# Attention 2 of a two-layer graph kernel: four destination blocks a turn in place of two, and another use of PSUM

## Chip, core and metric

The kernel runs on one core of a Trainium2 chip. The metric is the device time of one execution in microseconds (us). A core has a matrix engine (TensorE, PE in the profile, with its weight loads as PEld), VectorE (DVE), ScalarE (ACT), GpSimd (POOL) and SyncE (SP, which here only issues transfers). Each works through its own list of instructions in a fixed order, and waits at an instruction until what it needs is there.

## What is computed

Two pre-norm residual layers over a graph of 6250 nodes with 128 features and 200000 edges sorted by destination. The first layer is a two-stage graph attention network; the second a convolution over edges. The part that matters here is the second attention stage, with one head (feat has 64 columns before W2):

```python
feat = (x @ W).reshape(num_nodes, H, D)
el = jnp.sum(feat * attn_l[None], axis=-1)
er = jnp.sum(feat * attn_r[None], axis=-1)
e = jax.nn.leaky_relu(el[src] + er[dst], NEG_SLOPE)
ee = jnp.exp(e - m[dst])
s = jax.ops.segment_sum(ee, dst, num_segments=num_nodes)
msg = feat[src] * (ee / s[dst])[:, :, None]
rst = jax.ops.segment_sum(msg, dst, num_segments=num_nodes)
```

then `x = x + rst`, a layer norm, a ReLU, and two linear maps of the result for the convolution.

## The kernel before

Nodes are cut into 49 blocks of 128 (NB). The program has three stages one after the other: tables, edge counts and attention 1 (0 to 2430 us of the profiled execution), attention 2 (2430 to 3014 us), and the convolution (from 3014 us to the end).

Attention 2 is dense. Attention 1 has left in DRAM, for each destination block, a matrix of edge counts: how many edges run from each of the 6272 sources to each of its 128 destinations. The leaky ReLU has two branches, so each count is split in two: `up` where el + er is positive, `down` where it isn't. Then `up` and `down`, as weights, are multiplied with two prepared tables (`rhs2`, 196 columns each: three bf16 pieces of 65 values, and a column of ones that counts edges).

The loop before (from line 1156) takes two destination blocks a group, 25 groups (24 of two blocks, one of one). A group does this:

- SP loads the counts `ct` of both blocks for all 49 source blocks, 8 transfers of 392 KB (line 1162).
- PE spreads er over the partitions (`pe`, line 1164, one small PSUM bank of two in `ps_sm`), and ACT copies it to `erb` (line 1167, two buffers).
- Seven steps, each over 7 source blocks (HS). In a step ACT makes 7 `ramp` rows of 256 columns (line 1181: Relu of erb times 2^60 plus a bias, so 0 or huge), DVE makes `up` as the smaller of ramp and count (1185) and `down` as count minus up (1186), and PE multiplies 28 weights of 128x128 with 196 columns (1190), `up` first for both blocks, then `down`. `ramp`, `up` and `down` have two buffers each.
- The sums stand in a tile `big` of two banks (two buffers, so four banks), and DVE takes them out with four instructions a block (1198 to 1202).

After every second group `finish2` (lines 1105 to 1151) is made for the four blocks just done. It is a generator of nine pieces, of which one is taken after each step of the groups that follow, so that its work is spread between theirs: shares on DVE (512 to 515), transposes of g on PE (312) with a copy on ACT (314), a product with W2 (1115), the sum into `xt` on DVE (1116), norm statistics (291, 292), a root on ACT (301), eight `h` on ACT (1127, 1128), and, twice for two blocks each, transposes (312), a copy on DVE (314), a product with `lin` (1136), a copy to `t3` on ACT (1139) and two updates of `xt` a block on DVE (1144, 1146). Its end is two writes by SP (table3 at 1150, xtd at 1151). Its PSUM comes from the one bank of `ps_bank`.

PSUM has eight banks: four for `big`, two for `ps_sm`, one for `ps_bank`, one kept for sums elsewhere. In the second group `load_inputs` (1092 to 1094) loads x into `xt` and lets POOL add a bias to all of it; in the fifth `load_tiles` brings two tables for the convolution. The convolution's first gather from table3 can start once the last `finish2` has been written.

The order of instructions on each engine is not that of the source: a scheduler of the framework sorts them when the program is built, by its own estimate of when each can start. Buffers that are reused become waits. So where an instruction stands in its engine's list has to be read from the built program.

Of the kernel before, what the change touches and what calls it, by code (L numbers as in the profile page):

```python
# [30 lines left out]
F32 = mybir.dt.float32  # L31
# [11 lines left out]
P = 128  # L43
# [23 lines left out]
def gnn_kernel(ctx: ExitStack, tc: tile.TileContext, x, src, dst, attr4, attr8,  # L67
# [978 lines left out]
    ps_big = ps_two.enter_context(tc.tile_pool(name="ps_big", bufs=2, space=PSUM))  # L1046
    ps_sm = ps_two.enter_context(tc.tile_pool(name="ps_sm2", bufs=2, space=PSUM))
    ps_bank = ps_two.enter_context(tc.tile_pool(name="ps_bank2", bufs=1, space=PSUM))
# [50 lines left out]
    with tc.tile_pool(name="att2", bufs=1) as pool, tc.tile_pool(name="dense", bufs=2) as dense, \  # L1099
# [54 lines left out]

        behind = iter(())
        for b0 in range(0, NB, 2):
            n = min(2, NB - b0)
            ct = dense.tile([P, 2, NQ, NB, QN], BF16, name="ct")
            pe = small()
            for k in range(n):  # L1160
                for quarter in range(NQ):
                    (nc.sync if k == 0 or b0 else nc.scalar).dma_start(
                        ct[:, k, quarter].rearrange("p h d -> p (h d)"), counts[b0 + k][quarter])
                nc.tensor.matmul(pe[:, k * P:(k + 1) * P], er2[:, b0 + k, :].to_broadcast([P, P]), ident,
                                 start=True, stop=True)
            erb = dense.tile([P, 2 * P], F32, name="erb")
            nc.scalar.copy(erb[:, :n * P], pe[:, :n * P])
            if b0 == 0:
                for h0 in range(0, NB, HS):
                    nc.sync.dma_start(rhs2[:, h0:h0 + HS], rhs2d[:, h0:h0 + HS])  # L1170
            if b0 == 2:
                load_inputs()
            acc = big().rearrange("p (k a) c -> p k (a c)", k=2)
            if b0 == 8:
                load_tiles(pool)
            for h0 in range(0, NB, HS):
                ramp = dense.tile([P, HS, 2 * P], BF16, name="ramp")
                up = dense.tile([P, HS, 2 * P], BF16, name="up")
                down = dense.tile([P, HS, 2 * P], BF16, name="down")
# [3 lines left out]
                c = ct[:, :n, :, h0:h0 + HS, :].rearrange("p k a h d -> p h (k a) d")  # L1183
# [3 lines left out]
                for j, m in ((0, up), (1, down)):  # L1187
                    for h in range(HS):
                        for k in range(n):
                            nc.tensor.matmul(acc[:, k, j * C2:(j + 1) * C2], m[:, h, k * P:(k + 1) * P],  # L1190
                                             rhs2[:, h0 + h, j, :],
                                             start=h0 + h + j == 0, stop=h0 + h + j == NB)
                next(behind, None)
            parts = dense.tile([P, 2, 2, R2], F32, name="parts")
            acc = acc[:, :n, :2 * C2].rearrange("p k (j c) -> p k j c", j=2)
            for k in range(n):
                b = b0 + k
                nc.vector.tensor_reduce(parts[:, k], acc[:, k, :, :3 * R2].rearrange("p j (s f) -> p j f s", s=3),
                                        axis=AX.X, op=OP.add)
                nc.vector.tensor_reduce(deg[:, b:b + 1], acc[:, k, :, C2 - 1], axis=AX.X, op=OP.add)  # L1200
                nc.vector.tensor_scalar(parts[:, k, 1, :], parts[:, k, 1, :], pq2[:, b, 1:2], None, op0=OP.mult)
                nc.vector.scalar_tensor_tensor(acc2[:, b, :], parts[:, k, 0, :], pq2[:, b, 0:1], parts[:, k, 1, :],
                                               op0=OP.mult, op1=OP.add)
            if b0 % 4 == 2 or b0 + n == NB:
                deque(behind, 0)
                behind = finish2(b0 // 4 * 4, b0 + n - b0 // 4 * 4)
# [6 lines left out]
        def all2():  # L1213
            load_inputs()
            for b0 in range(0, NB, 4):
# [274 lines left out]
```

## Time and profile before

| what | value |
|---|---|
| runs of the kernel | 5505.89, 5550.96, 5581.69 us; median 5550.96 |
| profiled execution, its own time | 5588.02 us |
| its span, first to last instruction | 5586.3 us, mean granted TensorE clock 0.72 |
| busy in attention 2, 2430 to 3014 us (584 us) | ACT 543.5, PE 502.6, PEld 451.5, DVE 481.0, POOL 14.0 us |
| granted TensorE clock in that stretch | 0.96 (0.68 before it, 0.70 after it) |
| transfers in that stretch | 164 GB/s, 48% of the 16 transfer engines |
| ramps (line 1181) | 1225, 491.8 us busy |
| pair products (line 1190) | 4802, 480.2 us busy |
| `up` and `down` (lines 1185, 1186) | 175 each, 386.4 us busy |

Busy times of PE overlap with themselves, since matmuls are pipelined and each is counted with its way through the array. In the views, "[idle before <-releaser]" is the time an engine stood still ahead of an instruction and what ended it; xN is a number of instructions merged into a row.

### The profile page before, as it was taken

Reading aid. Unit: us, or ns where it says so; the run is one execution under the profiler, and the core shown is the slowest. Engines: PE = TensorE matmul, PEld = TensorE weight load, DVE = VectorE, ACT = ScalarE, POOL = GpSimd, SP = SyncE. Lnnn points to the kernel's source line nnn. Section 1 sums busy time; section 2 is a strip of 40 time slices with the busy share of each in tenths; the row PEclk is TensorE's granted clock in tenths of the full one; section 3 lists DMA queues with packets and bytes.
Section 4 is the critical chain, followed back from the end, with each engine's and each line's share of the span. In section 5 each row is a group of like instructions: output and inputs, shape, how many; then the busy total and the mean of one; then the engine's idle time right before and its main releaser. Section 6 shows DMA issues by size and latency. Waiting matters only on the chain. (4 is left out here: it accounts for less than half of the span.)

```text
span 5586.3 us, 66809 instructions
## 1 busy us (share of the span) xinstructions
PE 3395.3 (61%) x22075; PEld 2519.0 (45%) x22076; DVE 3498.1 (63%) x5531; ACT 2900.8 (52%) x6921; POOL 2639.6 (47%) x2684
## 2 busy tenths in 40 slices
PE   3124554644555545569995566676667666677676
PEld 2124444544444445558884334344434344444444
DVE  4255555655656655668885566666666666666667
ACT  2024655754655656669995344444444444444444
POOL 2655545545345445310003555555556556555553
PEclk9998555655666556669997676767767666767667
DMA  4243433433334434454442111111111111111111
GB/s 105 60 125 98 120 109 110 137 104 108 110 113 118 118 101 118 115 188 151 163 165 70 45 48 47 46 49 48 48 47 49 46 48 49 48 47 49 47 48 30
DMA packets 348033, 480.97 MB, mean 86 GB/s; under 512 B 190602, under 2 KB 236208, under 8 KB 343695
## 3 DMA queue, kind: packets, MB, share of 16 engines
q1 hardware_dynamic: 199014, 238.86, 14.2%
q0 software_dynamic: 85776, 147.31, 11.2%
q10 hardware_dynamic: 62872, 90.28, 4.6%
q8 instruction: 181, 2.97, 0.2%
q14 instruction: 190, 1.55, 0.1%
HBM read 367.21 MB, written 108.97 MB: 85 GB/s over the span
## 5 line engine op out<-in xcount | busy, mean ns | idle before, releaser
L319 POOL DMA_INDIRECT G<-table,srcc x1563 | 1475.4, 944 | 1556.8 <-issue 676.6
L319 POOL DMA_INDIRECT G<-table,srcw x1054 | 1091.9, 1036 | 987.3 <-DVE w L362 384.4
L1300 PE MATMUL whole<-halves,ohr 128*128 128x512 f32 x1563 | 798.7, 647 | 24.3 <-issue 23.3
L885 ACT ACTIVATE ramp<-erb,sel 128x256 bf16<-128x256 f32 x1764 | 756.5, 499 | 1.9 <-DVE up L887 1.6
L1252 ACT ACTIVATE hid<-big 128x512 f32<-128x512 f32 x392 | 233.9, 597 | 951.5 <-PE big L1250 419.5
L780 ACT CAST ca<-small 128x392 bf16<-128x392 f32 x784 | 350.2, 482 | 644.3 <-remote 413.0
L778 PE MATMUL small<-key,lo 128*128 128x98 bf16 x3136 | 339.0, 260 | 484.3 <-ACT ca L780 213.3
L1300 PEld LDWEIGHTS whole<-halves,ohr 128*128 128x128 f32 x1563 | 418.1, 283 | 438.2 <-issue 373.7
L1250 PE MATMUL big<-a8t,wm_sb 16*128 16x512 f32 x392 | 294.5, 840 | 394.8 <-issue 346.6
L1274 ACT ACTIVATE g<-G,a 128x128 f32<-128x128 f32 x1563 | 506.9, 401 | 11.2 <-DMA G<-table,srcc 9.6
L1181 ACT ACTIVATE ramp<-erb,sel 128x256 bf16<-128x256 f32 (+1 forms) x1225 | 491.8, 499 | 23.5 <-DVE up L1185 16.8
L778 PEld LDWEIGHTS <-lo 128*128 128x128 bf16 x3136 | 262.4, 128 | 533.5 <-issue 523.0
L767 DVE TENSOR_TENSOR lo<-slots,turned 128x2048 bf16<-128x2048 bf16 x196 | 239.5, 1222 | 418.5 <-remote 206.0
L1293 DVE TENSOR_TENSOR halves<-mess,halves 128x1024 fp32r<-128x1024 f32 x196 | 239.1, 1220 | 350.6 <-ACT halves L1287 201.2
L1250 PE MATMUL big<-hid,wm_sb 128*128 128x512 f32 x392 | 356.7, 1011 | 112.4 <-ACT hid L1252 99.0
L905 PE MATMUL up<-rc,up 128*128 128x102 bf16 x3528 | 323.5, 268 | 144.8 <-DVE up L887 106.4
L1258 PE MATMUL big<-wtp_sb,hid 64*128 64x128 f32 x3126 | 289.4, 331 | 142.6 <-issue 79.0
L1258 PEld LDWEIGHTS big<-wtp_sb,hid 64*128 64x128 f32 x3126 | 244.2, 229 | 246.9 <-issue 140.0
L377 PE MATMUL whole<-halves,ohr 128*128 128x136 f32 x1054 | 248.1, 388 | 173.1 <-issue 80.0
L905 PEld LDWEIGHTS <-up 128*128 128x128 bf16 x3528 | 272.9, 131 | 176.5 <-DVE up L887 127.3
L887 DVE TENSOR_TENSOR up<-ramp,ctc 128x1792 bf16<-128x1792 bf16 x252 | 273.8, 1087 | 97.2 <-ACT ramp L885 64.2
L377 PEld LDWEIGHTS whole<-halves,ohr 128*128 128x128 f32 x1054 | 218.3, 294 | 185.2 <-issue 84.5
(294 smaller groups left out, 6252.9 us busy)
## 6 DMA issues: line engine op xcount, KB each, us to landing
counts<-ca ACTq DMA_DIRECT2D x196, 392.0 KB
ct<-counts SPq DMA_DIRECT2D x192, 392.0 KB
rc<-rhs SPq DMA_DIRECT2D x63, 717.5 KB
oht<-dlow SPq DMA_DIRECT2D x31, 1088.0 KB
ctc<-counts SPq DMA_DIRECT2D x504, 56.0 KB
G<-table,srcc POOLq DMA_INDIRECT x1563
G<-table,srcw POOLq DMA_INDIRECT x1054
a8t<-attr_rows SPq DMA_DIRECT2D x391, 16.0 KB
```

The source lines that it names most:

```text
L319: nc.gpsimd.indirect_dma_start(out=G[:, c, :], out_offset=None, in_=table, in_offset=bass.IndirectOffsetOnAxis(ap=idx[:, c:c + 1], axis=0))
L377: nc.tensor.matmul(acc, oh[:, c, :], ms[:, c].rearrange("e s f -> e (s f)"), start=start and c == 0, stop=stop and c == n - 1)
L778: nc.tensor.matmul(ps[:, k * NKEY:(k + 1) * NKEY], lo[:, a, :, r], ky[:, a, :, r], start=True, stop=True)
L780: nc.scalar.copy(ca[:, :, i * W:(i + WBANK) * W].rearrange("p h (k d) -> p h k d", d=W), ps[:, :WBANK * NKEY].rearrange("p (k h d) -> p h ...
L885: nc.scalar.activation(ramp[:, i, :n * P], erb[:, h, :n * P], AF.Relu, bias=sel1[:, h0 + i, h:h + 1], scale=STEEP)
L887: nc.vector.tensor_tensor(up[:, :, :n * P].rearrange("p h (a d) -> p h a d", d=QN), ramp[:, :, :n * P].rearrange("p h (a d) -> p h a d", d ...
L905: nc.tensor.matmul(ups[k][:, h], up[:, i, k * P:(k + 1) * P], by_head[:, i, :, h, :], start=h0 + i + h == 0, stop=h0 + i + h == NB + H1 - 2)
L1181: nc.scalar.activation(ramp[:, h, :n * P], erb[:, :n * P], AF.Relu, bias=sel2[:, h0 + h, :], scale=STEEP)
L1250: nc.tensor.matmul(ph, w, (hid[-1] if j else x)[:, :npr * P], start=True, stop=True)
L1258: nc.tensor.matmul(pw[:, c, :], hid[1][half, j * P:(j + 1) * P], wtp_sb[half].rearrange("x p u -> x (p u)"), start=True, stop=True)
L1274: nc.scalar.activation(g0[:, c], G[:, c, :], AF.Copy, scale=a0[:, c, :])
L1300: nc.tensor.matmul(acc, oh[:, c, :], ms[:, c].rearrange("e s h i u -> e (s h i u)"), start=start, stop=stop)
```

## The change

Attention 2 is cut otherwise. All edits are between the pools of the stage and its end.

- Groups, called turns, have four blocks; block 0 alone goes first (49 = 1 + 12 x 4), where the odd block was last before. `ramp`, `up`, `down` and `erb` have 512 columns; `erb` has one buffer.
- The counts come in three pieces a turn, of 21, 21 and 7 source blocks, into two buffers of 21.
- PSUM: three tiles of two banks for sums (`ps_pair`, two of them a turn), and one bank (`ps_sm`, which is also `ps_bank`) for everything else: `pe`, and all of `finish2`.
- A step's products go block by block (7 `up`, 7 `down`, then the next block), each half of a bank.
- The sums are taken out two blocks at a time with four instructions (`leave`), written in the source after the first `up` and `down` of the next turn; then `finish2` of the turn just ended is begun, and two of its pieces are taken a step.
- The seven loads of rhs2 alternate between the queues of SP and ACT; the loads of x and of the tables stand in turns 1 and 2.

```diff
-    ps_big = ps_two.enter_context(tc.tile_pool(name="ps_big", bufs=2, space=PSUM))
-    ps_sm = ps_two.enter_context(tc.tile_pool(name="ps_sm2", bufs=2, space=PSUM))
-    ps_bank = ps_two.enter_context(tc.tile_pool(name="ps_bank2", bufs=1, space=PSUM))
+    ps_pair = ps_two.enter_context(tc.tile_pool(name="ps_pair", bufs=3, space=PSUM))
+    ps_bank = ps_sm = ps_two.enter_context(tc.tile_pool(name="ps_sm2", bufs=1, space=PSUM))
...
+        cols = 4 * P
+        blocks = [(b, min(4, NB - b)) for b in range(NB % 4, NB, 4)]
+        blocks = [(0, NB % 4)] * (NB % 4 > 0) + blocks
+
+        PIECE = 3 * HS
+        assert NB % HS == 0
+
+        def load_counts(b0, n, h0):
+            m = min(PIECE, NB - h0)
+            ct = dense.tile([P, 4, NQ, PIECE, QN], BF16, name="ct")
+            for k in range(n):
+                for quarter in range(NQ):
+                    nc.sync.dma_start(ct[:, k, quarter, :m].rearrange("p h d -> p (h d)"),
+                                      counts[b0 + k][quarter, :, h0 * QN:(h0 + m) * QN])
+            return ct
+        def leave(b0, n, accs):
+
+            for k0 in range(0, n, 2):
+                m = min(2, n - k0)
+                bs = slice(b0 + k0, b0 + k0 + m)
+                acc = accs[k0 // 2][:, :m].rearrange("p k (j c) -> p (k j) c", j=2)
+                parts = dense.tile([P, 4, R2], F32, name="parts", bufs=1)
+                nc.vector.tensor_reduce(parts[:, :2 * m], acc[:, :, :3 * R2].rearrange("p q (s f) -> p q f s", s=3),
+                                        axis=AX.X, op=OP.add)
+                nc.vector.tensor_reduce(deg[:, bs], acc[:, :, C2 - 1].rearrange("p (k j) -> p k j", j=2),
+                                        axis=AX.X, op=OP.add)
+                nc.vector.tensor_tensor(parts[:, :2 * m], parts[:, :2 * m],
+                                        pq2[:, bs, :].rearrange("p k j -> p (k j)")[:, :, None].to_broadcast([P, 2 * m, R2]),
+                                        op=OP.mult)
+                by_block = parts[:, :2 * m].rearrange("p (k j) f -> p k j f", j=2)
+                nc.vector.tensor_add(acc2[:, bs, :], by_block[:, :, 0], by_block[:, :, 1])
         behind = iter(())
-        for b0 in range(0, NB, 2):
-            n = min(2, NB - b0)
-            ct = dense.tile([P, 2, NQ, NB, QN], BF16, name="ct")
+        gone = None
+        for turn, (b0, n) in enumerate(blocks):
+            ct = load_counts(b0, n, 0)
             pe = small()
             for k in range(n):
-                for quarter in range(NQ):
-                    (nc.sync if k == 0 or b0 else nc.scalar).dma_start(
-                        ct[:, k, quarter].rearrange("p h d -> p (h d)"), counts[b0 + k][quarter])
                 nc.tensor.matmul(pe[:, k * P:(k + 1) * P], er2[:, b0 + k, :].to_broadcast([P, P]), ident,
                                  start=True, stop=True)
-            erb = dense.tile([P, 2 * P], F32, name="erb")
+            erb = dense.tile([P, cols], F32, name="erb", bufs=1)
             nc.scalar.copy(erb[:, :n * P], pe[:, :n * P])
-            if b0 == 0:
+            if turn == 0:
                 for h0 in range(0, NB, HS):
-                    nc.sync.dma_start(rhs2[:, h0:h0 + HS], rhs2d[:, h0:h0 + HS])
-            if b0 == 2:
+                    (nc.sync, nc.scalar)[h0 // HS % 2].dma_start(rhs2[:, h0:h0 + HS], rhs2d[:, h0:h0 + HS])
+            if turn == 1:
                 load_inputs()
-            acc = big().rearrange("p (k a) c -> p k (a c)", k=2)
-            if b0 == 8:
+            if turn == 2:
                 load_tiles(pool)
+            accs = None
             for h0 in range(0, NB, HS):
-                ramp = dense.tile([P, HS, 2 * P], BF16, name="ramp")
-                up = dense.tile([P, HS, 2 * P], BF16, name="up")
-                down = dense.tile([P, HS, 2 * P], BF16, name="down")
+                if h0 and h0 % PIECE == 0:
+                    ct = load_counts(b0, n, h0)
+                ramp = dense.tile([P, HS, cols], BF16, name="ramp")
+                up = dense.tile([P, HS, cols], BF16, name="up")
+                down = dense.tile([P, HS, cols], BF16, name="down")
                 for h in range(HS):
                     nc.scalar.activation(ramp[:, h, :n * P], erb[:, :n * P], AF.Relu,
                                          bias=sel2[:, h0 + h, :], scale=STEEP)
-                c = ct[:, :n, :, h0:h0 + HS, :].rearrange("p k a h d -> p h (k a) d")
+                i = h0 % PIECE
+                c = ct[:, :n, :, i:i + HS, :].rearrange("p k a h d -> p h (k a) d")
                 parts = [t[:, :, :n * P].rearrange("p h (a d) -> p h a d", d=QN) for t in (ramp, up, down)]
                 nc.vector.tensor_tensor(parts[1], parts[0], c, op=OP.min)
                 nc.vector.tensor_tensor(parts[2], c, parts[1], op=OP.subtract)
-                for j, m in ((0, up), (1, down)):
-                    for h in range(HS):
-                        for k in range(n):
-                            nc.tensor.matmul(acc[:, k, j * C2:(j + 1) * C2], m[:, h, k * P:(k + 1) * P],
+                if accs is None:
+                    if gone:
+                        leave(*gone)
+                        behind = finish2(*gone[:2])
+                    accs = [ps_pair.tile([P, 2, 512], F32, tag="pair", name="pair") for _ in range(0, n, 2)]
+                    gone = b0, n, accs
+                for k in range(n):
+                    for j, m in ((0, up), (1, down)):
+                        for h in range(HS):
+                            nc.tensor.matmul(accs[k // 2][:, k % 2, j * 256:j * 256 + C2], m[:, h, k * P:(k + 1) * P],
                                              rhs2[:, h0 + h, j, :],
                                              start=h0 + h + j == 0, stop=h0 + h + j == NB)
-                next(behind, None)
-            parts = dense.tile([P, 2, 2, R2], F32, name="parts")
-            acc = acc[:, :n, :2 * C2].rearrange("p k (j c) -> p k j c", j=2)
-            for k in range(n):
-                b = b0 + k
-                nc.vector.tensor_reduce(parts[:, k], acc[:, k, :, :3 * R2].rearrange("p j (s f) -> p j f s", s=3),
-                                        axis=AX.X, op=OP.add)
-                nc.vector.tensor_reduce(deg[:, b:b + 1], acc[:, k, :, C2 - 1], axis=AX.X, op=OP.add)
-                nc.vector.tensor_scalar(parts[:, k, 1, :], parts[:, k, 1, :], pq2[:, b, 1:2], None, op0=OP.mult)
-                nc.vector.scalar_tensor_tensor(acc2[:, b, :], parts[:, k, 0, :], pq2[:, b, 0:1], parts[:, k, 1, :],
-                                               op0=OP.mult, op1=OP.add)
-            if b0 % 4 == 2 or b0 + n == NB:
-                deque(behind, 0)
-                behind = finish2(b0 // 4 * 4, b0 + n - b0 // 4 * 4)
+                for _ in range(2 if h0 else 0):
+                    next(behind, None)
+            deque(behind, 0)
+        leave(*gone)
+        behind = finish2(*gone[:2])
         deque(behind, 0)
```

More of the change, by code (lines that the diff above doesn't have):

```diff
@@ L1214, in all2 @@
             load_inputs()
-            for b0 in range(0, NB, 4):
-                deque(finish2(b0, min(4, NB - b0)), 0)
+            for b0, n in blocks:
+                deque(finish2(b0, n), 0)
         def keep2(b, tot):
```

## The prediction, on record before the result

> **What bounds the stage now.** The page of the profile first: in its slices the stage is where ACT shows 9s and the granted clock too. Then the busy times of one stretch of the middle of attention 2, from one write of table3 to the next, which is one set of four blocks:
>
> ```profile
> core 0: us, PE busy (x) PEld busy (x) DVE busy (x) ACT busy (x) POOL busy (x), PEclk, DMA share, GB/s
> 2573.98:2617.70 43.72, 40.07 (x426) 36.23 (x425) 37.55 (x69) 43.72 (x113) 0.00 (x0) 1.00 0.47 163
> ```
>
> ACT is busy all 43.72 us, PE runs at the full clock, and all such sets take 43.7 us. So ACT is the bound. The waits of the stage agree (waiter, releaser: us in total, times, longest): DVE waits for ramps 58 times, PE for DVE, ACT almost for nobody.
>
> ```profile
> PEld L1190 <- DVE up L1185: 69.8, 84, 11.5
> DVE up L1185 <- ACT ramp L1181: 40.1, 58, 1.5
> ACT ramp L1181 <- DVE up L1185: 16.8, 4, 11.0
> ```
>
> Then the timeline, for the prices and for how a group hands over to the next:
>
> ```profile
> 2541.71 0.62 ACT L1167 COPY erb<-small 128x256 f32<-128x256 f32 x2
> ...
> 2545.37 0.64 PE L1164 MATMUL small<-ident,er 128*128 128x128 f32 x4
> ...
> 2967.31 11.69 ACT L1181 ACTIVATE ramp<-erb,sel 128x256 bf16<-128x256 f32 x29
> 2968.22 1.35 PE L1190 MATMUL big<-rhs,down 128*128 128x196 bf16 x14
> ...
> 2979.03 1.09 DVE L1185 TENSOR_TENSOR up<-ramp,ct 128x1792 bf16<-128x1792 bf16 x1 [0.51 <-ACT ramp L1181]
> 2979.17 9.16 ACT L1181 ACTIVATE ramp<-erb,sel 128x128 bf16<-128x128 f32 x31
> ...
> 2981.36 0.62 DVE L1185 TENSOR_TENSOR up<-ramp,ct 128x896 bf16<-128x896 bf16 x1
> ...
> 2982.56 0.75 PE L1190 MATMUL big<-rhs,up 128*128 128x196 bf16 x7
> ```
>
> Ramps follow each other every 0.399 us with 256 columns ((11.69-0.51)/28) and every 0.292 with 128 ((9.16-0.39)/30). A product costs 0.085 us ((1.35-0.25)/13), and also where seven in a row add to the same place (the x7 row). Two er spreads and two erb copies run together, for groups still ahead: ACT has the next group's erb before it needs it, and never stops.
>
> Last, PE's clock. After 5 us of idling its products start at half speed, 2.47 us for 14, twice in a row:
>
> ```profile
> 2467.34 2.47 PE L1190 MATMUL big<-rhs,up 128*128 128x196 bf16 x14 [4.77 <-DVE up L1185]
> 2469.60 2.49 PE L1190 MATMUL big<-rhs,down 128*128 128x196 bf16 x14
> 2471.89 1.69 PE L1190 MATMUL big<-rhs,up 128*128 128x196 bf16 x14
> ```
>
> **What the skill says.** "TensorE: Matmul & The Clock Gate", section "Part 1: The HAM clock gate (the "warmup" mystery)": an idle window of about 3.4 us halves PE's clock, and about as long a busy one restores it. The trace agrees: it was slow for 4.5 us (2467.3 to 2471.9). "SBUF — State Buffer", section "🔬 SBUF: two separate sides": DVE and POOL share a port pair that one holds for a whole instruction. Here too: an `up` took 13.72 us while POOL added to xt for 13.99. For the price of 512 columns, "ScalarE: Activation LUTs", section "What ACT_TABLE_LOAD costs": 280 + 0.833 N ns, 93 of them overlapped, an estimate of 0.614 us.
>
> **The change, part by part.**
>
> *Ramps.* 12 x 49 of 512 columns. From the two spacings, 0.107 per 128 columns, one costs 0.399 + 0.214 = 0.613 us, as the page has it. For four blocks 49 x 0.613 = 30.0 us in place of 98 x 0.399 = 39.1: 9 us of ACT saved, 109 in all.
>
> *up and down.* 0.47 us per 896 elements, so 3584 take 1.09 + 0.94 = 2.03 us: 14 x 2.03 = 28.4 against 28 x 1.09 = 30.5, 2 us of DVE saved.
>
> *Products.* The same 392 per four blocks, 392 x 0.085 = 33.3 us. With the PE work of finish2 (8 of L1136 at 0.28, 8 of L1115 at 0.125, 4 transposes of h at 0.17: 4.0 us) and 1.7 for er and g, PE needs 39 us. That is the floor of a turn.
>
> *Taking out sums.* Four instructions for two blocks in place of eight; per block L1198 to L1202 now take 0.56 + 0.15 + 0.25 + 0.28. I estimate 1.9 us a pair (a reduce of twice the size at 1.05, 0.15, then 0.42 as L515's equal size, 0.28). It lies on DVE beside ACT's work below: nothing. Without that cover it costs 3.8 us a turn.
>
> *Counts.* 588 transfers in place of 196, all on SP at some 0.46 us of issue (5 in 2.32 us). A piece of 2.75 MB is 7.4 us of issue, and as long to move at the 370 GB/s that the windows of 2530 to 2536 us show.
>
> *One bank for er and finish2, and one erb.* This decides. In the changed program's lists, PE's four er matmuls stand behind the last product of a turn (the bank is held by finish2 till then), ACT's erb copy behind all ramps of that turn, and DVE's `leave` ahead of the next `up`. So nothing of a turn starts before the last is finished. With E the end of a turn's last product:
>
> - er matmuls: E + 0.64;
> - erb, 512 columns (L314's copy of 512 takes 0.58): E + 1.3;
> - seven ramps, 6 x 0.613 + 0.7: E + 5.7;
> - first `up`: E + 7.8. DVE has long taken out the sums (E + 3.9);
> - first `down`, which PE wants after seven products: E + 9.9;
> - the other 49 products, 4.2 us: E + 14.1. But PE has idled since E + 0.64, but for four transposes of g near E + 3, so its clock is at half for some 4.5 us from E + 10: 27 products cost 0.082 more, 2.2 us: E + 16.3.
>
> Steps 1 to 6 are then PE's: 6 x 56 x 0.085 = 28.5, and finish2's 4.0: E + 48.8. In step 3 PE stops for the transposes of h. Step 3's `up` needs step 1's buffer, free at E + 20.7, so: up 22.7, xt sum 23.4, down 25.5, statistics 27.3, root 27.6, four ramps 30.1, first h 30.8. PE is there at 16.3 + 2.5 x 4.75 + 1.0 = 29.2 and waits 1.6. A turn is **50.5 us** (48.5 if the clock holds; 52 if it stays half through step 0) against 43.72 for four blocks now.
>
> *Start.* Before, the stage starts at 2430. After, I count 13.1 MB until turn 1 can begin (counts 1.6 and 2.75, rhs2 4.8, x 3.2, a table 0.8), 35 us at the 373 GB/s that the window of 2430 to 2464 us shows, so about 2467, then the collision with POOL: first `up` of turn 1 done near 2478, as if E were 2470. Three loads of rhs2 now stand on ACT ahead of the first ramps, 3 us (7 such issues took 7.04), inside a start that waits for transfers anyway. The first finish2 has one block: 2.5 us less.
>
> *End.* Now the last, one-block finish2 is open, 17 us from the last product (2997) to the first gather (3014). After, a whole one of four blocks is: by the same rows 3.0 until g, 6 to the xt sum, 2.8 statistics and root, then h, transpose, lin and t3 twice, 9, writes and restart 4.7: 25.5 us.
>
> **Sum.** After: 40 + 12 x 50.5 - 2.5 + 25.5 = 669 us for the stage; now 584 (3014 - 2430). So 85 us more. On the profiled execution's own 5588.02 that is 5673; the runs' median is 5550.96, 37 below it, so I forecast **5636 us**, 1.5% more. Nothing outside the stage is touched in the lists.
>
> **What goes the other way, and what hides.** The counts of the next turn's first piece can be asked for when `down` of step 5 is done: its buffer is free when PE ends step 3 (E + 33.5), and `up` and `down` take 4.2, so E + 37.8. In SP's list 11 of its 16 transfers stand ahead of the two writes of finish2, which wait for t3 and xt (near E + 45, since the last product with lin comes in the middle of step 5); with the other five it is all there by about E + 49.5. It is wanted at E' + 5.7 = E + 56: hidden, by 6.5 us, and only because of the gap. Behind those writes on SP stand the second piece (wanted in step 3, 13 us later than it can land) and the third.
>
> **Rivals.**
> - *The saved ramps show.* If the handover overlapped (er early, as now), a turn falls to PE's 39 us: 12 x 39 + 3.5 against 12 x 43.72 is -53, 5498 us. For it: ACT is the bound now. Against: the lists. Between this and my chain lies a warm PE without the wait for h, a turn of 46.5 us and 5588. Together 0.18.
> - *The clock stays down* through steps 0 and 1, since PE stops between its first seven products and the first `down`, which may spoil the busy window. Then 105 products are slow in place of 27: +6.4 us less the 1.6 of the wait, a turn of 55.5, 5696 us, slower by 2.6%. It decides from 52.7 us a turn. For it: bursts with gaps; against: every slow spell of the trace ended after 4.5 us. 0.15.
> - *The counts come late:* if a piece takes 8 us longer than its cushion, 12 x 8 more, 5732 us. For it: rows of 1344 bytes in place of 3136, and the writes in SP's way. 0.10.
> - Forecast, 5600 to 5680: 0.57.
>
> **Numbers.** Runs of this kernel differ by 1.4%, and about 2% is what a measurement can tell from no change: 111 us. From 5555 (which leaves out half of the first rival, 0.09) to 5715 (the clock's case inside, the counts' 0.10 outside) 2 in 10 are left out. Slower by over 2% (above 5662): both late rivals, 0.25, and the top of the forecast, 0.07. Faster by over 2% would need 34 us a turn, below PE's floor: 0.02. The rest, 0.66, is within 2%.
>
> **What would show it.** Writes of table3 some 50 us apart; ACT idle about 6 us a turn ahead of the erb copy, released by PE; PE idle over 4 us ahead of a turn's first product, released by `up`, and 2.4 us for the next 14; DVE never long waiting for `ct`. Wrong, if the er matmuls run ahead of a turn's last product, if `up` waits for a transfer each turn, or if the clock shows 0.5 for a whole step.

## The result and the profile after

The changed kernel took 5608.61 us (median of four runs, 5581.64 to 5632.0), the kernel before 5550.09 us: 1.0118 times as long, with a 95% interval of 1.0074 to 1.0162, so 41 to 90 us more. The profiled execution of after (5581.64 us) happens to be the quickest of its four, that of before (5588.02 us) is slower than all four that it is compared with here, and attention 1, which the change doesn't touch, ended 44 us earlier in that of after. So only lengths of the stage are compared, from the first er matmul to the first gather of the message stage (the prediction counted from 2430, 1.5 us later; its start is given on this scale):

| | before | after | forecast for after |
|---|---|---|---|
| start, to where turn 1 can be said to begin (its first `up` done, less 8.1) | | 46.3 | 41.5 |
| twelve turns of four blocks, to the last product | | 579.9 | 603.5 |
| open end, to the first gather | | 27.8 | 25.5 |
| stage | 586.0 | 654.0 | 670.5 |
| one turn of four blocks in the middle | 43.7 | 48.4 | 50.5 |

The stage is 68 us longer, within the interval of the runs. One turn in the busy times of after, to be read beside the line of before:

```profile
core 0: us, PE busy (x) PEld busy (x) DVE busy (x) ACT busy (x) POOL busy (x), PEclk, DMA share, GB/s
2906.97:2955.34 48.37, 40.85 (x427) 38.48 (x426) 36.29 (x48) 34.88 (x62) 0.00 (x0) 0.93 0.49 144
```

ACT fell from 43.72 to 34.88 us: the saving of 9 us is there. But nobody is busy all the time any more; PE, the busiest, works 40.85 of 48.37 us, and its mean granted clock is 0.93. The waits of eight turns say for whom:

```profile
ACT erb L1197 <- PE small L1194: 68.3, 8, 8.8
ACT t L1138 <- PE bank L1135: 39.6, 8, 5.0
PE pair L1229 <- DVE up L1218: 38.0, 8, 5.0
DVE up L1218 <- DMA ct<-counts: 23.6, 7, 3.4
```

Once a turn ACT waits 8.5 us for the er matmuls, DVE for something that the view calls ct, and PE 4.7 us for `up`. The timeline of one boundary shows these three as one chain:

```profile
2809.90 0.28 DVE L1145 SCALAR_TENSOR_TENSOR xt<-bank,xt 128x96 f32<-128x96 f32 x1
...
2816.01 0.75 PE L1229 MATMUL pair<-rhs,down 128*128 128x196 bf16 x7
2816.60 1.08 PE L1194 MATMUL small<-ident,er 128*128 128x128 f32 x8
2817.78 0.59 ACT L1197 COPY erb<-small 128x512 f32<-128x512 f32 x1 [8.50 <-PE small L1194]
2818.40 8.68 ACT L1213 ACTIVATE ramp<-erb,sel 128x512 bf16<-128x512 f32 x14
2822.82 2.02 DVE L1218 TENSOR_TENSOR up<-ramp,ct 128x3584 bf16<-128x3584 bf16 x1 [3.38 <-DMA ct<-counts]
2824.88 2.02 DVE L1219 TENSOR_TENSOR down<-ct,up 128x3584 bf16<-128x3584 bf16 x1
2824.90 1.98 PE L1229 MATMUL pair<-rhs,up 128*128 128x196 bf16 x11 [4.72 <-DVE up L1218]
2826.96 1.15 PE L1229 MATMUL pair<-rhs,down 128*128 128x196 bf16 x7
2827.95 0.75 PE L1229 MATMUL pair<-rhs,up 128*128 128x196 bf16 x7
```

With E = 2816.76, the end of the last product, the er matmuls end at E + 0.9, erb at E + 1.6, the seventh ramp at E + 6.0 (2818.40 + 6 x 0.613 + 0.7), the first `up` at E + 8.1, the first `down` at E + 10.1. Two more things are to be seen. The first line is finish2's last read of the small bank: it ends at E - 6.6, and ACT's 8.50 us of waiting begin at E - 7.5. Both the bank and ACT were free long before the er matmuls ran. And 11 products take 1.98 us, 0.17 each in place of 0.085; but the first `down`, which comes next in PE's list, is made only at 2826.90, when the 11 are just done: PE lost next to nothing by being slow there.

### The profile page after: what moved, and what is told of

It reads as the page before. It is cut to its first block, busy times and chain, and to the rows that moved or that the text cites. A ratio compares the mean times of both kernels' runs of the same rounds, so it can differ in the third digit from the quotient of the medians.

```text
span 5579.8 us, 66335 instructions
## 1 busy us (share of the span) xinstructions
PE 3389.7 (61%) x22075; PEld 2525.7 (45%) x22076; DVE 3479.4 (62%) x5267; ACT 2791.3 (50%) x6321; POOL 2636.7 (47%) x2684
## 5 line engine op out<-in xcount | busy, mean ns | idle before, releaser
L1330 PE MATMUL whole<-halves,ohr 128*128 128x512 f32 x1563 | 811.8, 656 | 12.7 <-issue 10.0
L1330 PEld LDWEIGHTS whole<-halves,ohr 128*128 128x128 f32 x1563 | 425.0, 286 | 434.9 <-issue 369.1
L778 PE MATMUL small<-key,lo 128*128 128x98 bf16 x3136 | 334.6, 259 | 467.9 <-issue 220.9
L778 PEld LDWEIGHTS <-lo 128*128 128x128 bf16 x3136 | 262.3, 128 | 510.5 <-issue 498.9
L1213 ACT ACTIVATE ramp<-erb,sel 128x512 bf16<-128x512 f32 (+1 forms) x637 | 381.1, 684 | 31.2 <-DVE up L1218 18.0
L1288 PE MATMUL big<-wtp_sb,hid 64*128 64x128 f32 x3126 | 272.4, 317 | 99.0 <-ACT hid L1282 52.8
L1229 PE MATMUL pair<-rhs,up 128*128 128x196 bf16 x2401 | 278.7, 258 | 86.4 <-DVE up L1218 77.6
L1288 PEld LDWEIGHTS big<-wtp_sb,hid 64*128 64x128 f32 x3126 | 229.2, 216 | 204.9 <-issue 98.5
```

What stands on the lines that cost most here:

```text
L778: nc.tensor.matmul(ps[:, k * NKEY:(k + 1) * NKEY], lo[:, a, :, r], ky[:, a, :, r], start=True, stop=True)
L1213: nc.scalar.activation(ramp[:, h, :n * P], erb[:, :n * P], AF.Relu, bias=sel2[:, h0 + h, :], scale=STEEP)
L1229: nc.tensor.matmul(accs[k // 2][:, k % 2, j * 256:j * 256 + C2], m[:, h, k * P:(k + 1) * P], rhs2[:, h0 + h, j, :], start=h0 + h + j == 0, ...
L1288: nc.tensor.matmul(pw[:, c, :], hid[1][half, j * P:(j + 1) * P], wtp_sb[half].rearrange("x p u -> x (p u)"), start=True, stop=True)
L1330: nc.tensor.matmul(acc, oh[:, c, :], ms[:, c].rearrange("e s h i u -> e (s h i u)"), start=start, stop=stop)
```

## Experiments

In all of them the mean length of a turn (or of four blocks) is the mean distance of the writes of table3 over nine or ten turns, the start left out. A write can be issued early or late, so where single turns are compared, the distance of their last products is taken. The runs fell on four chips. On two of them the kernel before takes 5546 or 5581 us, on the others 4425 and 4427; the difference lies outside this stage. So times are compared with the kernel before on the same chip. Lengths of turns agree much better: most turns of after and e2, and two long turns of e12 on a quick chip, take 48.36 to 48.38 us from last product to last product. Line numbers of other kernels are shifted by a few.

**e1: the er matmuls written earlier, same bank.**

```diff
...
+                if h0 == NB - HS and turn + 1 < len(blocks):
+                    following = spread(*blocks[turn + 1])
                 i = h0 % PIECE
```

`spread` makes the er matmuls and the erb copy of the next turn.

> The kernel after, with one thing moved: the er matmuls and the erb copy of the next turn are written in the program ahead of the up and down of the last step of a turn, not at the start of the next turn. Still one small bank, still one erb. In the changed program's list the er matmuls then stand about 112 products ahead of a turn's last product. My theory: what costs the 8 us between a turn's last product and the next turn's first is only the place of the er matmuls behind the last product; bank and erb are free some 6 us before that. Then the first up of a turn waits for the taking out of the first pair's sums and comes near E - 0.4 instead of E + 6.1, the first down near E + 2.6 (one reduce lies between), step 0 ends near E + 8.6 instead of E + 14.3, and a turn falls from 48.4 us to about 42.7, the whole by some 68 us to about 5540 us. If the counts of the next turn land only near E + 2, the turn is 45 us and the whole 5568. Rival one, the shared bank and the one erb themselves hold the handover: the er matmuls stop PE where they now stand until the bank is free, the turn stays within 1 us of 48.4 and the time near 5608. Rival two, counts: first up waits for ct each turn and the turn is 47 or more.

Measured: 5568.0 us, 1.0041 (1.0021 to 1.006) of the kernel before, so 36 of the 58 us are back; a turn is 45.0 us in the mean and 44.4 in half of them, the stage 618. I had expected 42.7 us and 5540, or 45 us and 5568 if the counts came late. The second pair of numbers came, but not for its reason: the first `up` below begins when the seventh ramp ends (2793.66 + 6 x 0.613 + 0.7 = 2798.04), not when counts land. Why a turn stays 1.7 us above the 42.7 was not followed up. One such turn, and its boundary (E = 2797.66):

```profile
core 0: us, PE busy (x) PEld busy (x) DVE busy (x) ACT busy (x) POOL busy (x), PEclk, DMA share, GB/s
2789.28:2833.68 44.40, 40.37 (x427) 37.80 (x425) 35.41 (x47) 35.00 (x62) 0.00 (x0) 0.96 0.54 157
```

```profile
2791.87 1.08 PE L1191 MATMUL small<-ident,er 128*128 128x128 f32 x8
2793.04 0.59 ACT L1194 COPY erb<-small 128x512 f32<-128x512 f32 x1 [3.79 <-PE small L1191]
2798.09 2.03 DVE L1225 TENSOR_TENSOR up<-ramp,ct 128x3584 bf16<-128x3584 bf16 x1 [0.98 <-DMA ct<-counts]
2800.17 2.47 PE L1236 MATMUL pair<-rhs,up 128*128 128x196 bf16 x14 [2.51 <-DVE up L1225]
2802.98 0.96 PE L1236 MATMUL pair<-rhs,down 128*128 128x196 bf16 x7 [0.34 <-DVE down L1226]
```

The er matmuls run 5.8 us before the last product instead of just behind it, everything else follows (up at E + 0.4 in place of E + 6.1), and the turn loses 4 us. With one bank and one erb. So in after neither held the er matmuls at run time: their place in PE's list did.

**e11, e6 and e3: the sharing alone, in the kernel before.** One bank for er and finish2 (e11), one erb (e6), both (e3); pairs of blocks, 256 columns and counts as before.

```diff
-    ps_sm = ps_two.enter_context(tc.tile_pool(name="ps_sm2", bufs=2, space=PSUM))
-    ps_bank = ps_two.enter_context(tc.tile_pool(name="ps_bank2", bufs=1, space=PSUM))
+    ps_bank = ps_sm = ps_two.enter_context(tc.tile_pool(name="ps_sm2", bufs=1, space=PSUM))
...
-            erb = dense.tile([P, 2 * P], F32, name="erb")
+            erb = dense.tile([P, 2 * P], F32, name="erb", bufs=1)
```

> The kernel before, with only the sharing taken over from the change: er spreads and finish2 use one PSUM bank with one buffer in place of two and one, and erb has one buffer in place of two. Pairs of blocks, 256 columns and whole rows of counts as before. In its list the er matmuls stand 112 to 240 products ahead of a group's last product. Theory place in the list: no gap, 43.7 us for four blocks as before (up to 45 where ACT's erb copy comes late), and 5551 us within 0.5%. Rival, sharing one bank and one erb costs the handover by itself: each group of two blocks gets a gap of at least 2.5 us (er, erb, seven ramps of 0.4, up 1.1 behind its last product, less what ran ahead), so 48.7 us or more for four blocks and 5610 us or more.

> The kernel before with one erb buffer in place of two; the PSUM banks stay as they were. e3_before_shared, one bank for er and finish2 and one erb, took 48.64 us for four blocks against 43.72. If the bank is what costs, four blocks stay at 43.7 us (within 0.4: ACT copies erb behind its last ramp and goes on); if the single erb does, they come near 48.

> The kernel before with one PSUM bank for er and finish2 in place of two and one, and two erb buffers as before. With e6_before_one_erb (44.45 us for four blocks) and e3_before_shared (48.64) it splits the cost of sharing. If the bank is the cause, four blocks take 47 to 48.6 us here; if bank and erb each are harmless and only both together cost, 44.5 or less.

Measured for four blocks: e3 48.64 us (whole 1.0116, 1.0079 to 1.0152), e11 48.44 (a single run), e6 44.48 (a single run). What I expected of e3 was wrong. Its rival came within a tenth, though not by its own sum: it let both handovers of four blocks pay 2.5 us, and in the trace one of the two pays 4 us. e6 came out 0.8 above 43.72, twice what I had allowed. The kernel before, given only the shared bank, gets turns as long as those of the changed one; that the two lengths agree so closely is chance, since e11 adds idling to 44.15 us of ACT's work and after adds it to PE's. The busy times of e11 and e6:

```profile
2785.56:2834.01 48.45, 41.66 (x424) 37.88 (x424) 38.05 (x69) 44.15 (x113) 0.00 (x0) 0.96 0.43 146
```

```profile
2225.94:2270.39 44.45, 39.97 (x424) 36.36 (x424) 37.69 (x69) 44.22 (x113) 0.00 (x0) 1.00 0.46 162
```

ACT's work is about 44.2 us in both; with one erb it is still the bound, with one bank 4.3 us of idling are added. The timeline of e3 shows where, at one of the two boundaries of four blocks:

```profile
2720.27 1.35 PE L1189 MATMUL big<-rhs,down 128*128 128x196 bf16 x14
2721.46 0.64 PE L1163 MATMUL small<-ident,er 128*128 128x128 f32 x4
2722.18 0.37 ACT L1166 COPY erb<-small 128x256 f32<-128x256 f32 x1 [4.04 <-PE small L1163]
```

It is the chain of after in small. I had read in the list of e3 that the er matmuls stand well ahead of a group's end; that holds for one boundary in two. At the other they stand between finish2's last transposes of h and its last products with lin, and these are at the group's end. With a shared bank the list has to fit the er matmuls in between two uses by finish2, and it puts them late.

**e12: the change with a bank of its own for er.** The counterpart in after: `pe = whole()`, the accumulator's bank, in place of `pe = small()`; nothing else.

> The kernel after with one thing changed: the er matmuls use a bank of their own (the accumulator's, unused in this stage); where they are written in the program, erb, counts and writes stay. In its list the er matmuls are now ahead of a turn's last product for two turns out of three; for the third they stand with those of the turn after it right at the boundary. If the shared bank is what put them behind the last product, turns with early er matmuls take 41 to 45 us (as in e4_own_bank_early, held by counts) and the third stays near 48: a mean of 44.5 to 46 us and 5575 to 5590 us where the kernel before is at 5550. If the bank has no part in it, every turn stays at 48.4.

Measured: 45.2 us a turn in the mean, the stage 617 us, 1.0083 (1.0061 to 1.0105) of the kernel before. From last product to last product the turns come in threes: one of 48.1 to 48.4 us, one of 44.7 to 45.2, one of 43.0 to 43.3. (The writes of table3 blur this: 46.3 to 47.0 for two in three, 42.9 to 43.3 for the third.) This is what was expected. Ahead of a long turn (here E = 2171.43) PE has the er matmuls of two turns behind its last product, and then the gap of after:

```profile
2171.26 1.08 PE L1194 MATMUL whole<-ident,er 128*128 128x128 f32 x8
2173.08 1.16 PE L1194 MATMUL whole<-ident,er 128*128 128x128 f32 x8 [0.73 <-ACT erb L1197]
...
2179.56 1.98 PE L1229 MATMUL pair<-rhs,up 128*128 128x196 bf16 x11 [4.78 <-DVE up L1218]
```

The first product comes at E + 8.1 there; at the other boundaries, where er was spread long before, at E + 0.1 to E + 2.9. So the sharing put the er matmuls late in the list, and their place in the list makes the gap.

**e7: PE kept busy across the gap**, to see what the slow clock costs in after.

```diff
+            if gone and n == 4:
+                idle = whole()
+                for _ in range(75):
+                    nc.tensor.matmul(idle[:, :C2], rhs2[:, 0, 0, :P], rhs2[:, 0, 0, :], start=True, stop=True)
```

> The kernel after with 77 extra products a turn of data that is there already, into the unused accumulator bank (nobody reads them), written between the er matmuls and the first product of a turn: 70 of them stand ahead of it, some 6 us of PE work in the 7 us in which it is idle. They keep PE's clock up. The prediction charged the slow clock with 2.2 us a turn: then a turn falls from 48.4 to about 46.2 us. My reading of the trace of after: 11 of the slow products run while PE waits for the first down anyway, so only some 0.4 us are lost and the turn is 47.8 to 48.1 us; it must not be longer than 48.6, or the extra products are themselves in the way.

Measured, in a single run: 48.06 us a turn in the mean and 47.96 in most, against 48.50 and 48.37 in after. (The loop makes 75 products; the 77 of the text came from counting the list.) The clock was at full speed:

```profile
2276.26:2324.22 47.96, 45.63 (x504) 43.30 (x502) 36.15 (x47) 35.00 (x62) 0.00 (x0) 1.00 0.49 146
```

```profile
2243.90 1.35 PE L1233 MATMUL pair<-rhs,up 128*128 128x196 bf16 x14 [0.34 <-DVE up L1222]
```

The first 14 products take 1.35 us, and yet step 0 ends at E + 13.7 (2249.5, with E = 2235.8) against E + 14.4 in after. Of these 0.7 us, 0.3 come from three more products that ran ahead of the first `down`. The whole turn is 0.4 us shorter, so the clock costs a turn of after 0.4 us at most, not 2.2.

**e2 and e10: are the counts late in after?** e2 issues finish2's two writes on POOL's queue (`nc.gpsimd.dma_start`), so that all 16 transfers of the next turn's first piece go out in a row. e10 takes pieces of 14 source blocks in three buffers (`PIECE = 2 * HS`, `bufs=3`), so that the first piece has a free buffer after step 3.

> The kernel after, with the two writes of finish2 (table3 and xtd) issued by POOL's queue in place of SP's, so that all 16 transfers of a turn's first piece of counts go out in one row when the buffer is free. The profile of after puts the 3.4 us ahead of a turn's first up down to the ct transfer. My theory: that label is only the later of two near-equal ends, the seven ramps end at the same instant, so the first up stays 6.1 us behind the turn's last product and a turn stays at 48.4 us (within 0.4). Rival, the counts come late: the up comes 2 to 3.4 us earlier and a turn falls to 45 to 46.4 us.

> The kernel after with only the pieces changed as in e8_three_pieces (14 source blocks, three buffers); er matmuls and bank as in after. The prediction held the counts for hidden behind the gap by 6.5 us. Then nothing changes here: a turn stays at 48.4 us (within 0.4), and ACT still idles 8.5 us ahead of the erb copy. If counts had a part in the first up of after, the turn falls.

Measured: 48.5 us a turn in e2, 48.8 in e10 (two turns of 49.9 and 50.5 among them), a single run each. Neither is shorter. And in e10 the waits still name ct:

```profile
ACT erb L1197 <- PE small L1194: 59.8, 7, 8.8
...
DVE up L1218 <- DMA ct<-counts: 22.1, 13, 3.7
```

```profile
2911.29 8.68 ACT L1213 ACTIVATE ramp<-erb,sel 128x512 bf16<-128x512 f32 x14
2915.72 2.03 DVE L1218 TENSOR_TENSOR up<-ramp,ct 128x3584 bf16<-128x3584 bf16 x1 [3.65 <-DMA ct<-counts]
```

`up` starts 4.43 us after the first of its ramps here and 4.42 in after, which is when the seventh ramp ends. The name ct is the label of a wait on several things; the ramps ended it. The trace of after also holds the landings: the 16 transfers of that first piece were issued from 2803.90 on, and the last of them landed at 2816.92, 5.9 us ahead of the `up` at 2822.82. The prediction had named an `up` that waits for a transfer each turn as a sign against it; read from the label alone, this would have misled.

**e4 and e5: what comes next when the handover is early.** e4 gives er its own bank, writes the er matmuls at step 3 and the erb copy behind the last ramps; e5 puts finish2's writes on POOL's queue as well.

```diff
...
+                if turn + 1 < len(blocks):
+                    if h0 == 3 * HS:
+                        pe = spread(*blocks[turn + 1])
+                    if h0 == NB - HS:
+                        following = row(*pe)
```

`spread` makes the er matmuls, now into `whole()`, and `row` the erb copy.

> The kernel after with the er matmuls of the next turn in a bank of their own (the accumulator's, unused in this stage), written at step 3, and the erb copy written ahead of the last step's up. In the list up of step 0 then stands ahead of both takings out of sums. Against e1_early_spread (44.4 us a turn, the er matmuls 6 us ahead of the last product because the bank is held by finish2 until then) this asks what the shared bank still costs. My theory: ACT has erb right after its last ramp, some 14 us ahead of the last product, so only counts and the buffers of up can hold the next first up. If the counts land about E - 3, a turn is about PE's own 40.4 plus 0.7 for the wait for h, 41 us, and the whole near 5530 us, 0.4% below the kernel before. If they land only near E + 0.4 (two writes stand among their 16 transfers), PE still waits 2.4 us and then for down, and the turn stays at 44 to 44.5 us, 5568 us as in e1_early_spread.

> As e4_own_bank_early, and the two writes of finish2 are issued by POOL's queue, so that nothing stands among the 16 transfers of a turn's first piece of counts; the taking out of sums is written after the products of the first block. If counts are what holds the first up once the handover is early, this turn is 41 us against 44 to 44.5 in e4_own_bank_early, and the whole near 5530 us. If e4_own_bank_early is at 41 already, there is no difference (within 0.3 us a turn). Rival, PE or its clock: a turn of 43 us or more in both.

Measured: e4 1.0048 (1.0032 to 1.0063) of the kernel before, 43.8 us a turn in the mean, past the first ones 41.9 to 45.4 from last product to last product, short and long in turn; e5 1.0057 (1.0038 to 1.0077), 44.6. A long turn of e4 begins like this:

```profile
2211.50 2.03 DVE L1231 TENSOR_TENSOR up<-ramp,ct 128x3584 bf16<-128x3584 bf16 x1 [6.93 <-DMA ct<-counts]
2213.59 0.76 PE L1242 MATMUL pair<-rhs,up 128*128 128x196 bf16 x7 [2.54 <-DVE up L1231]
```

Here ct is the real releaser: the ramps were done long before (ACT itself waits 7.3 us for this `up`), and the last transfer of the piece landed at 2211.19. Its first was issued at 2197.63, so from there to `up` it took 13.9 us, and PE stood 2.5 us. The turns of 41.9 to 42.8 us are those that PE begins without a stop. Moving the writes off SP did not help. In e5 the 16 transfers are issued within 7.7 us in place of 8.9, but from the first issue to `up` it is 13.6 us (2293.91 to 2307.54), as in e4: the writes among them were not what made the counts late.

**e8 and e9: the counts taken off too.** e8 is e4 with e10's pieces. e9 has the odd block last as well:

```diff
...
-        blocks = [(b, min(4, NB - b)) for b in range(NB % 4, NB, 4)]
-        blocks = [(0, NB % 4)] * (NB % 4 > 0) + blocks
+        blocks = [(b, min(4, NB - b)) for b in range(0, NB, 4)]
```

> As e4_own_bank_early, with the counts in pieces of 14 source blocks in three buffers in place of 21 in two (the same memory, 64 transfers a turn in place of 48). The first piece of the next turn then goes into a buffer that is free after step 3 of a turn, some 16 us ahead of the last product, not after step 5. In e4 and e5 the first up of a turn was released by ct at about E + 0.4. My theory: with the handover early, the counts are the next bound, and this takes them off: PE goes through, a turn is PE's 40.4 plus 0.7 for h, about 41 us in every turn, and the stage some 575 us (586 in the kernel before): 10 us or 0.2% faster than the kernel before. Rival: 64 transfers are too many for SP or the rows of 896 bytes too short, and a turn stays at 43.5 us or more.

> As e8_three_pieces, with the odd block as the last turn in place of the first, so that the finish2 of the last four blocks runs beside the products of the odd block and only a finish2 of one block is left open at the end, as in the kernel before. The open end of after was 28 us from the last product to the first gather, that of before 17. Expected: turns of 41 us, an end of 17 to 18 us, so 10 us less than e8_three_pieces and some 20 us or 0.4% faster than the kernel before, if the start with four blocks costs no more than the start with one.

Measured: e8 0.9977 (0.9961 to 0.9994) of the kernel before, 42.5 us a turn in the mean, the stage 588.5: not the 41 us in every turn that I expected. From last product to last product, past the first turns, there are two kinds, of 41.2 us (40.4 in the last) and of 44.1 to 44.4, and the granted clock parts them:

```profile
core 0: us, PE busy (x) PEld busy (x) DVE busy (x) ACT busy (x) POOL busy (x), PEclk, DMA share, GB/s
2777.02:2818.35 41.33, 38.71 (x428) 37.14 (x427) 36.03 (x47) 35.43 (x64) 0.00 (x0) 1.00 0.64 169
2818.18:2862.43 44.25, 41.97 (x428) 39.94 (x427) 36.12 (x48) 35.42 (x64) 0.00 (x0) 0.92 0.61 161
```

Each of the five long turns has one stretch of 6.83 us at half clock (2831.09 to 2837.92 in this one), the others have none. Where PE is the bound, a slow spell costs some 2.9 us, not next to nothing as in after.

e9 0.9971 (0.995 to 0.9993), turns of 41.45 in the mean, the stage 571.9 us against 586.0. Nearly all of its turns are 41.2 us from last product to last product, as in e8 at full clock; one of 44.1 has a slow spell. So of the 16.6 us by which its stage is shorter than that of e8, I estimate that 4 x 2.9 = 11.6 lie in the four fewer spells of this execution, and little in the order of the blocks. The open end was 24.1 us, not the 17 to 18 that I expected. Two turns of e9, and the largest of PE's waits over six:

```profile
2690.35:2731.53 41.18, 38.56 (x427) 36.99 (x425) 35.86 (x46) 35.28 (x63) 0.00 (x0) 1.00 0.65 170
2773.24:2813.87 40.63, 38.01 (x420) 36.45 (x419) 35.34 (x43) 34.74 (x63) 0.00 (x0) 1.00 0.67 176
```

```profile
PE bank L312 <- DVE g L515: 8.3, 6, 1.7
```

PE no longer waits for `up`; its clock is full in these turns, and the 1.7 us for g are the longest that is left. The saved ramps now show: ACT has 6 us to spare, PE is nearest to being the bound, and a turn is 2.3 us below the kernel before. e9 is quicker than the kernel before by 0.3%: some 30 us are won between the first and the last write of table3, 12 are lost at the start, where the first write comes 114 us after the first er matmul (102 in the kernel before), and 4 at the end. This adds up to the 14 us of the stage. But e8 came out 0.2% quicker with a stage that is 2.5 us longer, so differences this small in the whole time are not all the stage's.

## Why the prediction was right, and where it was off

- **The mechanism** was right: the er matmuls behind the last product, then erb, seven ramps, `up`, products, one after the other. Forecast E + 0.64, 1.3, 5.7, 7.8 and 9.9 for er, erb, ramps, `up`, `down`; measured E + 0.9, 1.6, 6.0, 8.1 and 10.1. The er matmuls took 1.08 us, not 0.64, which was the price for two blocks (x4; four blocks make x8); the rest is carried over. ACT's idling is 8.5 us a turn, not about 6.
- **Its reason** was half right. That "the bank is held by finish2 till then" is not what the chip showed: the bank was free from E - 6.6. Sharing it decides the order of the list (e11, e12), and the list decides the time (e1, with the bank still shared). One erb costs little (e6: 0.8 us).
- **The term that was mis-sized is the clock's**: 2.2 us forecast, some 0.4 measured. From the first `down` at E + 10.2 on, 45 products at 0.0845 us would end at E + 14.0; step 0 ends at E + 14.4, and e7, at full clock, saves 0.4 a turn. The forecast's 48.5 us "if the clock holds" is nearly what came. Two things were missed. The first products run at E + 8.1, not with `down` at E + 10, and PE then waits for `down` anyway, so most of their slowness costs nothing. And the forecast let the slow spell begin with the products. The granted clock was at half from 2820.97 to 2827.80, 6.83 us, and PE had no products until 2824.90. In the trace of before it was at half for 6.83 us too (2465.76 to 2472.59); the 4.5 us were only most of the part in which products ran. The Trainium skill's "TensorE: Matmul & The Clock Gate" (section "Part 1: The HAM clock gate (the "warmup" mystery)") puts its window at about 3.4 us and calls it free-running. The traces agree: the clock of a trace changes only at points that lie whole multiples of 3.41 us apart.
- **Steps 1 to 6** with finish2 and the wait for h: forecast 34.1 us, measured 34.0 (48.4 - 14.4).
- **Taking out sums**: 1.9 us a pair forecast, 0.97 + 0.15 + 0.43 + 0.29 = 1.84 measured, done at E + 1.8 and hidden as forecast. In e1, with the gap mostly gone, the second pair's first reduce stands between `up` and `down`, where PE waits.
- **Counts**: hidden in after (e2, e10). The first piece landed 5.9 us ahead of its `up`, against 6.5 forecast; that is at E + 0.2, and the forecast's "only because of the gap" is what e4 shows.
- **Start**: 46.3 us for 41.5. The first `up` of turn 1 could begin 41.9 us after the first er matmul, released by the counts as forecast, but for 38.5; and the collision with POOL made it last 12.49 us:

```profile
2423.85 13.41 POOL L1093 TENSOR_TENSOR xt<-xt,b_sb 128x6272 f32<-128x6272 f32 x1 [140.78 <-DMA ct<-counts]
2426.64 12.49 DVE L1218 TENSOR_TENSOR up<-ramp,ct 128x3584 bf16<-128x3584 bf16 x1 [13.21 <-DMA ct<-counts]
```

- **End**: 27.8 us for 25.5; the products with lin for two blocks took 2.07 us there, twice (1.13 in the middle of the stage), at a granted clock of 0.50 from 3015.53 on.
- **The sum**: the forecast stage is 16.5 us too long (turns 23.6 too long, start 4.8 and end 2.3 too short). The other 11 us between 5636 and 5608.61 lie in the level of the runs, which this trace doesn't explain.
- **The rivals**: counts late and the clock down for two steps did not happen. The argument against the second, that every slow spell of the trace ended after 4.5 us, did not hold by the granted clock: that of before was down for 13.65 us from 2479.41 on. "The saved ramps show" did not happen here, but its floor of 39 us was near the truth: PE works 38.0 to 38.6 us in a turn of e9, whose length is 40.6 to 41.2.

## What to carry to other kernels

When two jobs are made to share a buffer, ask not only how long each holds it but where the shared buffer puts the later job's instructions in its engine's list; a job that starts the next round must not end up behind the last work of this one. A saving on the bounding engine is worth nothing until the handover from round to round has been walked through with the same durations, and once it is mended, the next cover that the gap gave (here the counts) has to be paid for. A cost that runs while its engine would wait anyway is no cost: before a slow clock is charged, look at what the engine waits for next. The same slow clock cost 0.4 us a turn in after and 2.9 in e8, where PE had become the bound.

## What was not expected of the hardware

- PE's clock after a pause. In after, 4.7 us without work and the clock was at half at once. In e1 it was so after 2.51 us (14 products in 2.47 us). In e3, on e1's chip, 14 products after a pause of 2.93 us took 1.35 us, full speed, and only the next 14 were slow, 2.33 us. In e4, on another chip, 7 after 2.54 us took 0.76, full speed. So the length of the pause alone does not tell when the slow products come.

```profile
2678.02 1.35 PE L1189 MATMUL big<-rhs,up 128*128 128x196 bf16 x14 [2.93 <-DVE up L1184]
...
2679.21 2.33 PE L1189 MATMUL big<-rhs,down 128*128 128x196 bf16 x14
```

The granted clock explains it. In the traces it changes only at points of a grid of 3.41 us, and whether it falls at such a point goes with how much of the 3.41 us before it PE was busy. Here are the cells just before a fall in e1 and in e3, and two cells of e8, in which PE makes the same pauses (1.3 and 0.5 us) but the grid lies a little otherwise:

```profile
2796.60:2800.01 3.41, 1.06 (x13) 0.83 (x10) 2.39 (x3) 3.41 (x7) 0.00 (x0) 1.00 1.03 341
2675.97:2679.38 3.41, 1.36 (x17) 1.36 (x17) 2.51 (x6) 3.41 (x10) 0.00 (x0) 1.00 1.02 329
2827.68:2831.09 3.41, 1.60 (x17) 1.29 (x15) 3.24 (x6) 3.41 (x7) 0.00 (x0) 1.00 0.59 119
2786.72:2790.13 3.41, 1.72 (x16) 1.51 (x17) 3.24 (x6) 3.41 (x7) 0.00 (x0) 1.00 0.59 121
```

After the first three (PE busy 31, 40 and 47%) the clock falls to half, after the fourth (50%) it stays, as it did in e4 (49%, 2212.36 to 2215.77). In e3 the fall at 2679.38 comes between the two rows above. Over this stage in all fourteen traces, 112 of 113 falls follow a cell with PE busy under 48%, and only 5 of the 1977 cells after which the clock stayed are under it. That is read from the traces, where the ends of products are modelled; no run was made to test it.

- The same kernel takes 5546 to 5581 us on some chips and 4425 on others, with a mean granted clock of PE of 0.72 in the one kind and 0.79 in the other. Single operations agree (the add to xt on POOL took 13.41 us in after and 13.40 in e12). What differs is waiting outside this stage: ahead of the matmuls of L778 PE stood 220.9 us in after without a releaser that the profile shows; in e12, on a quick chip, no such time is listed there.
